# Which block of an attention group is summed by GpSimd and which goes to TensorE alone, and when the sum is closed

## The chip, the cores and the metric

The kernel runs on one core of one Trainium2 chip. The metric is device time in microseconds (us) of one launch. The core has five engines that run their own instruction streams in order and wait for each other by semaphores: TensorE (PE; its weight loads are listed apart as PEld), VectorE (DVE), ScalarE (ACT), GpSimd (POOL) and SyncE (SP). SyncE and GpSimd issue the data transfers (DMA) that matter here.

## The reference, cut to what matters

For each of 8 frames of 2048 rows and 256 channels: multi-head attention with 8 heads of 32 channels and a mask, then a feed-forward part, with three layer norms and residuals.

```
scores = einsum('fnhd,fmhd->fhnm', q, k) / sqrt(D)
scores = where(adj > 0, scores, -1e9)
attn   = softmax(scores, axis=-1)
t      = einsum('fhnm,fmhd->fnhd', attn, v)
x      = layernorm(x + t)
x      = layernorm(x + relu(x @ w1 + b1) @ w2 + b2)
out    = layernorm(x_in + x)
```

What the change touches is the softmax's denominator: for each query and head, the sum of the exponentials over all 2048 keys.

## The kernel before, in words

**Groups and blocks.** The 2048 queries of a frame are cut into 4 chunks of 512 (`qc`), the 8 heads into 2 halves of four (`g`), and the 2048 keys into 16 blocks of 128 (`mb`). A group is (`f`, `qc`, `g`); it has 16 blocks, and all groups together have 1024 blocks, the list `items`. The groups follow each other as qc 0 g 0, qc 0 g 1, qc 1 g 0, and so on.

**One block.** `scores` (L215, L218) makes the scores of 128 keys and 512 queries for four heads on TensorE, into two double banks of PSUM, and VectorE adds the mask while it moves them to a tile `p` of 128 x 2048 in SBUF. `exponentials` (L222) applies exp in place on ScalarE. `values` (L234) multiplies the tile by the values on TensorE and adds up over the 16 blocks in a bank. The main loop issues, at block t: `advance(t, 1)`, which runs pieces of side work; the exponentials of block t+1; the scores of block t+2; the values of block t; and `add_up` of block t. So a side piece stands ahead of the scores and the values of its block in TensorE's order. `advance` isn't called at block 0 of a group, and gives out one PSUM bank, so one TensorE piece, a block.

**The denominator.** The sum over the keys of a block is a product with a matrix of ones on TensorE. To save such products, the 16 tiles of a group are first added into a few. `add_up` does that with two means. The blocks in `POOLED` are added by GpSimd, one after the other, into the tile of block 0 (L256). The blocks in the two chains of `MOVED` are added by accumulating transfers that GpSimd issues (L253), each into the first tile of its chain; a later transfer of a chain adds into the same tile and waits until the earlier one has landed. One block, `ALONE`, is added to nothing. So four tiles, the terms, are left. `denominator` multiplies each with ones (L292, four matmuls a term, all accumulating in one bank), two terms in one piece of side work and two in the next; its result is turned (L299) and inverted. It begins `SUM` blocks after the last block of the group, that is in a block of the next group.

**What follows.** After g 1 of a chunk, `outcome` divides (L328, L329) and adds the input rows by an accumulating transfer (L317). `tail` follows: a norm, the feed-forward (L394, L397, L399, L405, L415, L417), a second norm with GpSimd's L339 and L341, the residual by an accumulating transfer (L343), and the third norm. Its GpSimd operations stand in the same queue as `add_up`'s. They start at blocks counted from `SUM`. Other side work prepares the next frame: rows are turned (L152), written to DRAM and loaded again (L182), and projected to queries, keys and values (L172, L197).

**Buffers.** The tiles `p` come from a pool of 11; a tile is reused when the values, the sum that takes it in, or the ones-product has read it. Side work is ordered by a list of start blocks and due times, and the whole order is fixed when the program is built.

In the last group of the program the blocks in `ENDED` aren't added by GpSimd but go to TensorE as terms of their own.

Of the kernel before, what the change touches and what calls it, by code (L numbers as in the profile page):

```python
# [55 lines left out]
def fast_path(ctx, tc, cst, x, adj, out, RS):  # L56
# [30 lines left out]
    def bank(dt=F32):  # L87
        shape = [P, CH] if dt == F32 else [P, 2, CH]
        if state["side"] is not None:
            i = 1 - state["side"]  # L90
            return ps_x[i].tile(shape, dt, name=f"x{i}")
        i = state["turn"]
        state["turn"] = (i + 1) % 5
        pool = ps_s[i] if i < 3 else ps_x[i - 3]
        return pool.tile(shape, dt, name=f"s{i}" if i < 3 else f"x{i - 3}")
# [109 lines left out]
    PT, O, OT, RC = {}, {}, {}, {}  # L205
# [33 lines left out]

    POOLED = (0, 3, 6, 8, 11, 13, 15)
    MOVED = ((1, 4, 7, 10), (2, 5, 9, 12))
    ALONE = 14

    ENDED = (13, 15)
    SUM = 4

    def add_up(item):
        f, qc, g, mb = item  # L250
        for chain in MOVED:
            if mb in chain[1:]:
                nc.gpsimd.dma_start(PT[f, qc, g, chain[0]], PT.pop(item), accum_op=ALU.add)  # L253
        if mb in POOLED[1:] and not ((f, qc, g) == items[-1][:3] and mb in ENDED):
            first = PT[f, qc, g, POOLED[0]]
            nc.gpsimd.tensor_tensor(first, first, PT.pop(item), ALU.add)  # L256
# [22 lines left out]

    def denominator(f, qc, g):  # L280
        grp = (f, qc, g)
        terms = [PT.pop((f, qc, g, ALONE))] + [PT.pop((f, qc, g, chain[0])) for chain in MOVED + (POOLED,)]
        if (f, qc, g) == items[-1][:3]:
            terms[3:3] = [PT.pop((f, qc, g, b)) for b in ENDED]
        yield BANK
        ps = bank()
        for n, term in enumerate(terms):
            if n == 2:
                yield BANK
            for h in range(4):  # L290
                r = D * h
                nc.tensor.matmul(ps[r:r + D, :], cst["ones"], term[:, h, :], start=(n == 0), stop=(n == len(terms) - 1))  # L292
        dT = op.tile([P, CH], F32, name="dT")
        nc.scalar.copy(dT, ps)  # L294
        yield 1
        yield BANK
        ps = bank()
        for j in range(TPC):
            nc.tensor.transpose(ps[:, j * P:(j + 1) * P], dT[:, j::TPC], ident)  # L299
        if g == 0:  # L300
            RC[f, qc] = op.tile([P, TPC, H], F32, name="rc")
        rc = RC[f, qc]
        den = ps.rearrange("p (j c) -> p j c", c=P)[:, :, ::D]
        nc.vector.reciprocal(rc[:, :, 4 * g:4 * g + 4], den)
        nc.vector.tensor_tensor(RS[:, 0], RS[:, 0], den, ALU.add)
        nc.vector.tensor_tensor(RS[:, 1], RS[:, 1], den, ALU.min)
        if g == 1:
            begin = items.index((f, qc, g, LAST)) + SUM + 2
            start(begin, outcome(f, qc) if (f, qc) != (F - 1, NCK - 1) else finish(f, qc), begin)

    def outcome(f, qc):
        yield ROOM
        state["tails"] += 1
        xin = x[f, qc * CH:(qc + 1) * CH, :].rearrange("(p j) c -> p j c", p=P)
        y = yp.tile([P, TPC, C], F32, name="y")
        yield from divide(f, qc, y)
        nc.gpsimd.dma_start(y, xin, accum_op=ALU.add)  # L317
        begin = items.index((f, qc, 1, LAST)) + SUM + 2
        start(begin + 10, tail(f, qc, y, xin), begin + 26)
# [13 lines left out]
    def tail(f, qc, y, xin):  # L333
        yield from norm(y)
        yield from feed_forward(y)
        yield 1
        z = y
        yield from norm(z)
        nc.gpsimd.tensor_tensor(z, z, rows(cst["g2r"]), ALU.mult)  # L339
        yield 1  # L340
        nc.gpsimd.tensor_tensor(z, z, rows(cst["be2r"]), ALU.add)  # L341
        yield 1
        nc.gpsimd.dma_start(z, xin, accum_op=ALU.add)  # L343
        yield 7
        yield from norm(z)
        nc.sync.dma_start(out[f, qc * CH:(qc + 1) * CH, :].rearrange("(p j) c -> p j c", p=P), z)
        state["tails"] -= 1
# [20 lines left out]
    def finish(f, qc):  # L368
        y = yp.tile([P, TPC, C], F32, name="y")
        xr, xb = state["rows"], take([P, TPC, C], F32)  # L370
        yield from divide(f, qc, y)
        nc.vector.tensor_tensor(y, y, xr, ALU.add)
        norm_halves(y)
        nc.vector.tensor_tensor(xb, xr, rows(cst["be2r"]), ALU.add)
        yield from feed_forward(y)
        z = y
        norm_halves(z)
        for h in range(0, TPC, 2):
            nc.vector.tensor_tensor(z[:, h:h + 2], z[:, h:h + 2], rows(cst["g2r"])[:, h:h + 2], ALU.mult)
            nc.vector.tensor_tensor(z[:, h:h + 2], z[:, h:h + 2], xb[:, h:h + 2], ALU.add)  # L380
        norm_halves(z)
        dst = out[f, qc * CH:(qc + 1) * CH, :].rearrange("(p j) c -> p j c", p=P)
        for h in range(0, TPC, 2):
            nc.sync.dma_start(dst[:, h:h + 2], z[:, h:h + 2])
# [37 lines left out]
    def start(t, gen, due):  # L422
        fill.append([t, gen, 1, due])
        fill.sort(key=lambda e: e[3])
# [88 lines left out]
    for t, (f, qc, g, mb) in enumerate(items):  # L513
        if mb == 0 and t:
            state["side"] = 1 - state["side"]
        if g == 1 and mb % 2 and (f + 1 < F or qc + 1 < NCK):
            load_mask(f + (qc + 1) // NCK, (qc + 1) % NCK, mb // 2)
        if f + 1 < F:
            for what, *which in NEXT.get((2 * qc + g, mb), []):
                due = t + MB // 2 if what is turn else items.index((f + 1, 0, which[1], which[0] * TPC)) - LEAD - 1  # L520
                start(t, what(f + 1, *which), due)
        if t == len(items) - MB // 2:
            state["rows"] = take([P, TPC, C], F32)
            nc.sync.dma_start(state["rows"], x[f, qc * CH:(qc + 1) * CH, :].rearrange("(p j) c -> p j c", p=P))
        if mb:
            advance(t, 1)

        if t + 1 < len(items):
            exponentials(items[t + 1])
        if t + LEAD < len(items):  # L530
            nf, _, ng, nmb = items[t + LEAD]
            t0 = t
            while (nf, nmb // TPC, ng) not in V:
                advance(t0, 1)
                t0 += 1
            scores(items[t + LEAD])
        values(items[t])
        add_up(items[t])
        if mb == LAST:
            start(t + SUM, denominator(f, qc, g), t)  # L540
    t = len(items)
# [129 lines left out]
def kernel(  # L671
# [56 lines left out]
    nc.gpsimd.memset(RS[:, 1], 1.0)  # L728

    fast_path(tc, cst, x, adj, out, RS)  # L730


# [49 lines left out]
```

## Time and profile before

| | |
|---|---|
| time | 3436.56 us, median of 3 runs (3432.72 to 3441.2) |
| span of the profiled run | 3439.1 us |
| mean granted TensorE clock | 0.990 |
| groups, blocks | 64, 1024 |
| accumulating transfers p<-p (L253) | 384 of 1024 KB, 10.1 us in the median from issue to landing |
| adds on GpSimd (L256) | 382, 4.9 us each |
| ones-products (L292) | 2064 matmul instructions, 244.9 us busy |

A row of the profile's groups reads: line, engine, operation, what it writes and reads, how often; then the busy time, the mean of one in ns, and after the bar the engine's idle time ahead of the group's instructions and what ended it. A row of the waits reads: engine, tile and line, then what it waited for, the sum in us, how often, and the longest. A row of a timeline reads: start and duration in us, engine, line, operation, what it writes and reads, how many were merged, and in brackets the idle time ahead of it. A transfer issued by GpSimd occupies it for the issue alone; the landing comes later.

### The profile page before, as it was taken

Reading aid. Unit: us, or ns where it says so; the run is one execution under the profiler, and the core shown is the slowest. Engines: PE = TensorE matmul, PEld = TensorE weight load, DVE = VectorE, ACT = ScalarE, POOL = GpSimd, SP = SyncE. Lnnn points to the kernel's source line nnn. Section 1 sums busy time; section 2 is a strip of 40 time slices with the busy share of each in tenths; the row PEclk is TensorE's granted clock in tenths of the full one; section 3 lists DMA queues with packets and bytes.
Section 4 is the critical chain, followed back from the end, with each engine's and each line's share of the span. In section 5 each row is a group of like instructions: output and inputs, shape, how many; then the busy total and the mean of one; then the engine's idle time right before and its main releaser. Section 6 shows DMA issues by size and latency. Waiting matters only on the chain. (4 is left out here: it accounts for less than half of the span.)

```text
span 3439.1 us, 54435 instructions
## 1 busy us (share of the span) xinstructions
PE 3179.1 (92%) x22036; PEld 1038.5 (30%) x22036; DVE 2731.0 (79%) x3203; ACT 2426.5 (71%) x1937; POOL 2586.7 (75%) x1357
## 2 busy tenths in 40 slices
PE   6989999999999999999999999999999999998995
PEld 5222332223322233222332323223332223322222
DVE  4788768887788877888788887888768887689885
ACT  3677767776677767777677776777767777677774
POOL 0577768887688776888678876787777877788885
PEclk8999999999999999999999999999999999999998
DMA  8678768778678777778777777687776787777774
GB/s 309 149 156 173 173 161 174 158 159 200 142 167 184 154 180 153 163 172 181 170 154 170 161 175 178 141 180 172 164 179 140 160 187 167 169 158 154 151 162 99
DMA packets 149298, 575.99 MB, mean 167 GB/s; under 512 B 14608, under 2 KB 67344, under 8 KB 99888
## 3 DMA queue, kind: packets, MB, share of 16 engines
q0 software_dynamic: 64560, 435.85, 63.2%
q1 hardware_dynamic: 83664, 135.30, 11.4%
q8 instruction: 174, 2.85, 0.3%
q10 hardware_dynamic: 816, 1.31, 0.1%
q14 instruction: 84, 0.69, 0.1%
HBM read 131.99 MB, written 37.75 MB: 49 GB/s over the span
## 5 line engine op out<-in xcount | busy, mean ns | idle before, releaser
L218 DVE TENSOR_TENSOR p<-s,mask 128x1024 f32<-128x1024 f32 x2048 | 2410.0, 1219 | 568.5 <-PE s L215 343.9
L222 ACT ACTIVATE p<-p 128x2048 f32<-128x2048 f32 x1024 | 1956.6, 1911 | 484.6 <-DVE p L218 371.2
L256 POOL TENSOR_TENSOR p<-p 128x2048 f32<-128x2048 f32 x382 | 1851.8, 4898 | 385.9 <-ACT p L222 383.4
L215 PE MATMUL s<-qT,kT 32*128 32x512 f32 x8192 | 1169.8, 641 | 184.9 <-DVE p L218 174.6
L234 PE MATMUL x<-p,v 128*32 128x512 f32 x8192 | 1091.8, 605 | 2.3 <-ACT p L222 2.3
L253 POOL DMA_DIRECT2D p<-p x384 | 385.6, 1024 | 376.0 <-DMA p<-p 188.4
L215 PEld LDWEIGHTS s<-qT,kT 32*128 32x128 f32 x8192 | 320.5, 183 | 822.3 <-DVE p L218 756.2
L234 PEld LDWEIGHTS x<-p,v 128*32 128x32 f32 x8192 | 161.1, 108 | 780.1 <-issue 211.5
L172 PE MATMUL x<-in,wqkv 128*128 128x512 f32 x472 | 235.2, 621 | 14.7 <-DMA in<-xd 14.1
L292 PE MATMUL x<-p,ones 128*32 128x512 f32 x2064 | 244.9, 592 | 1.9 <-DMA p<-p 1.9
L274 ACT ACTIVATE y<-y,nb,rs 128x256 f32<-128x256 f32 x372 | 219.0, 590 | 7.1 <-POOL nb L271 7.1
L263 DVE BATCH_NORM_STATS2 st<-y 128x6 f32<-128x256 f32 x372 | 155.4, 418 | 0.0
L172 PEld LDWEIGHTS x<-in,wqkv 128*128 128x128 f32 x472 | 80.2, 189 | 170.9 <-issue 112.7
L294 ACT COPY dT<-x 128x512 f32<-128x512 f32 x64 | 37.4, 585 | 126.3 <-PE x L292 126.3
L415 PE MATMUL x<-w2s,hT 128*128 128x256 f32 x504 | 125.5, 392 | 0.1
L405 PE MATMUL x<-turned,w1s 128*128 128x512 f32 x248 | 123.0, 618 | 0.0
L197 PEld LDWEIGHTS x<-wqkv,in 128*128 128x128 f32 x896 | 104.2, 191 | 47.0 <-issue 41.1
L197 PE MATMUL x<-wqkv,in 128*128 128x128 f32 x896 | 114.9, 281 | 0.0
L292 PEld LDWEIGHTS x<-p,ones 128*32 128x32 f32 x2064 | 66.8, 110 | 156.4 <-issue 151.0
L415 PEld LDWEIGHTS x<-w2s,hT 128*128 128x128 f32 x504 | 90.6, 189 | 62.0 <-issue 50.3
L268 POOL TENSOR_TENSOR rs<-rs,mhalf 128x4 f32<-128x4 f32 x93 | 96.2, 1035 | 7.8
L200 ACT COPY v<-x 128x512 f32<-128x512 f32 x58 | 33.9, 585 | 93.6 <-PE x L197 93.6
(114 smaller groups left out, 1467.6 us busy)
## 6 DMA issues: line engine op xcount, KB each, us to landing
p<-p POOLq DMA_DIRECT2D x384, 1024.0 KB, 10.1
mask<-md SPq DMA_DIRECT2D x248, 128.0 KB, 6.2
y<-in_x_dram POOLq DMA_DIRECT2D x62, 512.0 KB, 6.1
in<-xd SPq DMA_DIRECT2D x59, 512.0 KB, 10.9
p<-in_adj_dram SPq DMA_DIRECT2D x16, 1024.0 KB, 9.6
out_dram<-y SPq DMA_DIRECT2D x31, 512.0 KB, 6.4
in<-in_x_dram SPq DMA_DIRECT2D x29, 512.0 KB, 10.4
xd<-in SPq DMA_DIRECT2D x28, 512.0 KB, 9.2
```

What stands on the lines that cost most here:

```text
L172: nc.tensor.matmul(ps, wqkv[:, a, k0:k0 + P], xT[:, a, :], start=(a == 0), stop=(a == 1))
L197: nc.tensor.matmul(ps[:, j * P:(j + 1) * P], xT[:, a, j * P:(j + 1) * P], wqkv[:, a, 2 * C + g * P:2 * C + (g + 1) * P], start=(a == 0), s ...
L215: nc.tensor.matmul(ps2[half][:, j, :], KT[f, mb // TPC, g][r:r + D, (mb % TPC) * P:(mb % TPC + 1) * P], QT[f, qc, g][r:r + D, :], start=Tr ...
L218: nc.vector.tensor_tensor(pt[:, 2 * half:2 * half + 2, :], ps, MK[f, qc, mb // 2][:, mb % 2, None, :].to_broadcast([P, 2, CH]), ALU.add)
L222: nc.scalar.activation(PT[item], PT[item], AF.Exp, scale=1.0 / math.sqrt(D))
L234: nc.tensor.matmul(O[grp][r:r + D, :], V[f, mb // TPC, g][:, mb % TPC, r:r + D], PT[item][:, h, :], start=(mb == 0), stop=(mb == LAST))
L253: nc.gpsimd.dma_start(PT[f, qc, g, chain[0]], PT.pop(item), accum_op=ALU.add)
L256: nc.gpsimd.tensor_tensor(first, first, PT.pop(item), ALU.add)
L263: nc.vector.bn_stats(st, t[:, j, :])
L274: nc.scalar.activation(t[:, j, :], t[:, j, :], AF.Identity, bias=nb[:, j:j + 1], scale=rs[:, j:j + 1])
L292: nc.tensor.matmul(ps[r:r + D, :], cst["ones"], term[:, h, :], start=(n == 0), stop=(n == len(terms) - 1))
L415: nc.tensor.matmul(ps[:, (j - jj) * C:(j - jj + 1) * C], hT[:, d, j * P:(j + 1) * P], w2s[:, d, :], start=(d == 0), stop=(d == 1))
```

## The change

```diff
-    POOLED = (0, 3, 6, 8, 11, 13, 15)
-    MOVED = ((1, 4, 7, 10), (2, 5, 9, 12))
-    ALONE = 14
-
-    ENDED = (13, 15)
-    SUM = 4
+    POOLED = (0, 3, 5, 8, 10, 12, 14)
+    MOVED = ((1, 4, 7, 11), (2, 6, 9, 13))
+    ALONE = 15
+
+    ENDED = (12, 14)
+    SUM = 3
...
-        terms = [PT.pop((f, qc, g, ALONE))] + [PT.pop((f, qc, g, chain[0])) for chain in MOVED + (POOLED,)]
+        terms = [PT.pop((f, qc, g, ALONE))] + [PT.pop((f, qc, g, chain[0])) for chain in (MOVED[0], POOLED, MOVED[1])]
         if (f, qc, g) == items[-1][:3]:
-            terms[3:3] = [PT.pop((f, qc, g, b)) for b in ENDED]
+            terms[2:2] = [PT.pop((f, qc, g, b)) for b in ENDED]
```

The last block of a group, 15, now goes to TensorE alone, and GpSimd's last add is that of block 14. The chains of transfers are cut anew: one ends in block 11 instead of 10, the other in block 13 instead of 12. With `SUM` 3 the ones-products stand in blocks 2 and 3 of the next group instead of 3 and 4, and what is counted from `SUM` moves one block earlier with them. The order of the terms changes: before it was the lone block, first chain, second chain, GpSimd's sum; now it is the lone block, first chain, GpSimd's sum, second chain. The purpose is to close the sum of a group earlier, and so to hand back the tiles of its first blocks earlier. The number of adds, transfers and products stays the same.

## The prediction

> **What bounds the kernel now.** I read the page's busy shares first, then its costliest groups, then the waits, then the GpSimd and TensorE timelines of one group.
>
> ```profile
> PE 3179.1 (92%) x22036; PEld 1038.5 (30%) x22036; DVE 2731.0 (79%) x3203; ACT 2426.5 (71%) x1937; POOL 2586.7 (75%) x1357
> ...
> L218 DVE TENSOR_TENSOR p<-s,mask 128x1024 f32<-128x1024 f32 x2048 | 2410.0, 1219 | 568.5 <-PE s L215 343.9
> ...
> L256 POOL TENSOR_TENSOR p<-p 128x2048 f32<-128x2048 f32 x382 | 1851.8, 4898 | 385.9 <-ACT p L222 383.4
> ...
> p<-p POOLq DMA_DIRECT2D x384, 1024.0 KB, 10.1
> ```
>
> TensorE leads, but a block has two paces. A block without a side piece takes two VectorE adds, 2 x 1.22 = 2.44 us (2.5 in the trace); a block with a side piece (ones-products, projection, feed-forward) takes 3.8 to 4.0 us of TensorE: 1.14 scores + 1.07 values + 1.7 to 1.9 of the piece. The 53.7 us average of 64 groups is a sum of such blocks with little idle. So moving a piece gains or loses nothing of itself; only a wait in TensorE's or VectorE's order changes the time. GpSimd is next: does it deliver sums in time?
>
> ```profile
> POOL p L253 <- DMA p<-p: 188.4, 43, 6.2
> ...
> PE x L292 <- DMA p<-p: 1.9, 1, 1.9
> ```
>
> GpSimd waits 188 us for the accumulate transfers of its own chains, but the ones-products (L292) nearly never wait. To see how much slack hides this, GpSimd in frame 2, group (qc 1, g 0):
>
> ```profile
> 1029.33 4.58 POOL L256 TENSOR_TENSOR p<-p 128x2048 f32<-128x2048 f32 x1 [3.15 <-ACT p L222]
> ...
> 1044.34 0.90 POOL L317 DMA_DIRECT2D y<-in_x_dram  x1
> 1044.96 1.19 POOL L253 DMA_DIRECT2D p<-p  x1
> 1045.54 5.21 POOL L256 TENSOR_TENSOR p<-p 128x2048 f32<-128x2048 f32 x1
> 1050.05 1.52 POOL L253 DMA_DIRECT2D p<-p  x1
> 1055.38 0.85 POOL L253 DMA_DIRECT2D p<-p  x1 [3.81 <-DMA p<-p]
> 1055.96 4.86 POOL L256 TENSOR_TENSOR p<-p 128x2048 f32<-128x2048 f32 x1
> 1060.48 2.66 POOL L339 TENSOR_TENSOR y<-y,g2r 128x1024 f32<-128x1024 f32 x1
> 1062.79 1.19 POOL L253 DMA_DIRECT2D p<-p  x1
> 1063.40 2.98 POOL L341 TENSOR_TENSOR y<-y,be2r 128x1024 f32<-128x1024 f32 x1
> 1065.73 5.17 POOL L256 TENSOR_TENSOR p<-p 128x2048 f32<-128x2048 f32 x1
> 1070.23 1.52 POOL L343 DMA_DIRECT2D y<-in_x_dram  x1
> 1070.99 9.90 POOL L256 TENSOR_TENSOR p<-p 128x2048 f32<-128x2048 f32 x2
> ```
>
> and TensorE at the start of the next group:
>
> ```profile
> 1069.21 1.07 PE L234 MATMUL x<-p,v 128*32 128x512 f32 x8
> 1070.94 1.14 PE L215 MATMUL s<-qT,kT 32*128 32x512 f32 x8 [0.67 <-DVE p L218]
> 1072.02 1.07 PE L234 MATMUL x<-p,v 128*32 128x512 f32 x8
> 1072.90 1.90 PE L292 MATMUL x<-p,ones 128*32 128x512 f32 x16
> ...
> 1076.68 1.90 PE L292 MATMUL x<-p,ones 128*32 128x512 f32 x16
> ```
>
> The exponential of block 15 ended at 1063.37 (call it E15). The last transfer (block 12, issued 1062.79) landed at 1070.33, 7.0 after E15; its term, the third, starts at 13.3 after E15: 6 us of slack. The last add (block 15, 1070.99 to 1076.5) ends 13.1 after E15, for the fourth term at 14.3 (1.90/2 = 0.95 a term): 1 us of slack.
>
> **What the Trainium skill says.** *DMA: Bandwidth & Descriptors*, section "SWDGE vs HWDGE vs iDMA": an accumulate in a transfer goes through GpSimd's software path alone, and that has one queue. The trace agrees: two accumulates issued at 1083.13 and 1083.75 landed after 6.9 and 13.7 us, one behind the other. *TensorE: Matmul & The Clock Gate*, "The mechanism": matmuls start and end strictly in program order, so a late ones-product holds the scores behind it; no run here shows the hold at length (1.9 us once, above). *GPSIMD Engine Reference*, "Elementwise": a two-input add of 2048 fp32 columns takes 4497 ns; here 4534 at least, 4868 in the median, and I use the trace.
>
> **The change, part by part.** Same counts: 6 adds, 6 accumulate transfers and 4 terms of 4 matmuls a group. (a) Ones-products move from blocks 3 and 4 to 2 and 3, and all that is queued behind them one block earlier: cost 0 by the additive block times. (b) The buffer that comes free latest relative to its next use: the new order lets every block's buffer be reused 8 blocks on, where some had 6 and 7. No row of the waits shows VectorE held by it beyond about 20 us in all, so I give it 0 to 10 us. (c) Both chains now have gaps of 3 and 4 blocks instead of some 3 and 3. (d) The second chain ends in block 13, not 12, and its term is the fourth, in block 3.
>
> Part (d) decides. For a group like the one above I set E3 = 0. With the pieces a block earlier, E4, E5 ... are the old intervals from E4 on: 4.1, 7.2, 10.2, 13.1, 16.0, 18.4, 20.9, 23.6, 26.1, 28.6, 31.2, and E15 = 33.7 (1065.87 - 1032.14). GpSimd's new order is add 3, transfer 4, a normalisation's four small operations, add 5, L317, transfers 6 and 7, add 8, transfer 9, add 10, L339, transfer 11, L341, add 12, L343, transfer 13, add 14. Add 5 starts 0.6 after E5, as add 6 does now behind the same operations, and ends 12.3. L317 issues then and lands 5.6 later as now, 17.9. Transfer 6, queued behind it, takes the 4.9 us that a queued accumulate takes in this stage (median over 112): 22.8. Transfer 9 must wait for it (same chain): issued 23.3. From there the operations follow back to back as from 1055.38 to 1070.23 above, with the same members: add 10 at 23.9, L343 at 23.9 + (1070.23 - 1055.96) = 38.2, transfer 13 at 39.0, add 14 from 39.6 to 45.
>
> L343's half megabyte lies directly ahead of transfer 13 in the one queue: it lands about 5.9 after issue (6.3 median, 5.8 least), at 44.1. Transfer 13 lands 4.9 (this stage) to 6.0 (median of the queued ones in g 1 groups, where mask loads share the engines) later: 49.0 to 50.1, so 15.3 to 16.4 after E15. The terms now start one block (1072.02 - 1069.21 = 2.8) earlier: 6.7, 7.6, 10.5, 11.4 after E15. Term 2 needs transfer 11 (issued 30.7, landed 37.6, 3.9 after E15): no wait. Term 3 needs add 14 (11.3): 0.8. Term 4 needs transfer 13: in all 3.9 to 5.0, I take 4.6; from the outside, 0.8 if L343 costs the queue nothing (39.0 + 6.9 alone) and 6.4 if both run at the slowest of their kind. Queued behind term 4 are the scores of block 5, and VectorE, ScalarE and the values wait for those. VectorE has one block of work at most, which it would have had anyway; it already waits for TensorE in these blocks, so the wait is paid in full.
>
> How many groups: those with g 0 have this tail work on GpSimd and short blocks at the end. qc 0, 1, 2 of 8 frames, less the first (no tail yet), and qc 3 of the last frame: 24. In the 8 with qc 2 a projection lengthens a late block, and their last add lags 6.7 instead of 7.8 now, so 3.5 each. 16 x 4.6 + 8 x 3.5 = 102 us. In g 0, qc 3 the last blocks take 4 us, so GpSimd catches up (transfer 13 about 7 after E15, term 4 at 14.7). In g 1 groups blocks are long too: transfer 13 about 5 to 11 after E15 for a term at 13 or later.
>
> Gains: VectorE's L417 waits 22.3 us in all for GpSimd's L399; in the new g 1 groups L399 ends some 4 us ahead of need. Under half of those waits is on the path (VectorE has 0.9 us to spare in such blocks): 9 us. The end of the program: term 6 waits for the last transfer both before and after; 0. Sum: 3436.6 + 102 - 9 = 3530.
>
> **The rivals.** (1) A small stall: transfer 13 overtakes or shares with L343, 0.8 to 1 us x 24 = 22, less 9: 3450. For it: the page states no order of completion across engines; against: queued transfers landed one by one. Chance 0.14. (2) Faster: GpSimd is far enough ahead after the rearranged chains (188 us of its waits go) that no term waits, and the waits of (b), L417 and part of the reload stalls go: 3436 - 22 = 3415. For it: those waits are there; against: GpSimd's idle time isn't the path's, and L343 stays ahead of transfer 13. Chance 0.10. (3) Larger: 24 x 6.4 = 154, without gains: 3590. For it: some queued transfers in g 1 groups took 9.4; chance 0.10. My forecast: 0.66.
>
> **How the numbers follow.** The time is the forecast's, 3530. Range: 3455 (nearly rival 1) to 3580 (nearly rival 3) leaves out about 0.2. Faster than 0.3%: 0.10 (rival 2). Slower: forecast, rival 3 and most of rival 1: 0.86. Same: 0.04.
>
> **What would show it.** In the changed profile: the weight load or matmul of L292 waiting for DMA p<-p, some 24 times 3 to 6 us, about 100 us in all; it appears at block 3 of g 1 groups, after L343 and transfer 13 issued back to back; L417's waits for L399 shrink; GpSimd's waits for its own transfers fall below 188; plain blocks stay at 2.5. I am wrong if transfer 13 lands within 11.4 us of E15, or if L292's waits show and the group's length doesn't grow by them.

## The result and the profile after

The changed kernel takes 3565.95 us (median of 4 runs, 3560.19 to 3569.85) against 3435.72 of the kernel before on the same chip (4 runs, 3432.72 to 3441.2): ratio 1.0376, 95% interval 1.0354 to 1.0398, so some 130 us slower. The forecast was 3530, in a range of 3455 to 3580: direction and cause as forecast, the loss 37 us larger than the 93 forecast.

The page of the changed kernel, the lines that answer to those of before:

```profile
PE 3232.3 (91%) x22036; PEld 1040.8 (29%) x22036; DVE 2731.4 (77%) x3203; ACT 2426.6 (68%) x1937; POOL 2583.0 (73%) x1357
...
L256 POOL TENSOR_TENSOR p<-p 128x2048 f32<-128x2048 f32 x382 | 1834.9, 4803 | 595.2 <-ACT p L222 510.7
...
L292 PE MATMUL x<-p,ones 128*32 128x512 f32 x2064 | 262.3, 619 | 80.7 <-DMA p<-p 70.5
...
p<-p POOLq DMA_DIRECT2D x384, 1024.0 KB, 9.5
```

Counts are those of before, and VectorE, ScalarE and GpSimd are as busy in us as before. Two rows moved. The ones-products L292 now stand idle for `DMA p<-p`. And TensorE is busy 53 us longer (3232.3 against 3179.1) with the same 22036 matmuls, so some of them run slower. The mean granted TensorE clock is 0.975 (0.990 before).

The waits of the changed kernel (what waited and for what, sum in us, times, longest):

```profile
PEld x L292 <- DMA p<-p: 93.0, 25, 5.0
...
PE x L292 <- DMA p<-p: 70.5, 23, 4.1
...
POOL p L253 <- DMA p<-p: 54.0, 26, 4.3
```

The first two rows are one wait seen twice: the weight load of a term waits for its tile, and the matmul behind it waits along. They aren't to be added. The first begins while the matmuls of term 3 still run, the second, 70.5 us in 23 waits, is TensorE's idle time alone. GpSimd's waits for its own chains fell from 188.4 to 54.0 us, and the kernel is slower all the same.

GpSimd in the group that the prediction showed (frame 2, qc 1, g 0); block 15's exponential ends at 1088.47, which is E15:

```profile
1082.83 2.69 POOL L339 TENSOR_TENSOR y<-y,g2r 128x1024 f32<-128x1024 f32 x1
1085.14 1.20 POOL L253 DMA_DIRECT2D p<-p  x1
1085.77 2.98 POOL L341 TENSOR_TENSOR y<-y,be2r 128x1024 f32<-128x1024 f32 x1
1088.10 5.16 POOL L256 TENSOR_TENSOR p<-p 128x2048 f32<-128x2048 f32 x1
1092.60 1.51 POOL L343 DMA_DIRECT2D y<-in_x_dram  x1
1093.16 1.84 POOL L253 DMA_DIRECT2D p<-p  x1
1093.74 5.88 POOL L256 TENSOR_TENSOR p<-p 128x2048 f32<-128x2048 f32 x1
```

The chain of work that ended last, in the same stretch (start, us, what):

```profile
1092.60 0.56 POOL y L343
1093.16 11.31 DMA p<-p
1104.48 0.04 issue
1104.52 1.93 PE x L292 x8
```

L343's residual is issued just ahead of transfer 13. The transfer takes 11.3 us and lands at 1104.48, 16.0 after E15, while GpSimd's last add has been done since 1099.6. TensorE at that time:

```profile
1099.67 1.06 PE L292 MATMUL x<-p,ones 128*32 128x512 f32 x8 [0.25 <-POOL p L256]
1104.52 1.93 PE L292 MATMUL x<-p,ones 128*32 128x512 f32 x8 [3.78 <-DMA p<-p]
1106.38 2.09 PE L215 MATMUL s<-qT,kT 32*128 32x512 f32 x8
1108.40 1.94 PE L234 MATMUL x<-p,v 128*32 128x512 f32 x8
```

Term 3 takes 1.06 us. Term 4, after the idle time, takes 1.93 for the same eight instructions, and the scores and values behind it also take nearly double. The windows say why (us, busy time of PE, PEld, DVE, ACT, POOL, granted clock, DMA share, GB/s):

```profile
1100.80:1104.50 3.70, 0.00 (x0) 0.00 (x0) 0.12 (x1) 0.00 (x0) 3.53 (x4) 0.91 0.64 146
1104.50:1108.00 3.50, 3.48 (x16) 0.72 (x16) 0.00 (x0) 1.48 (x2) 1.54 (x1) 0.50 0.00 0
...
1112.00:1116.00 4.00, 4.00 (x34) 1.27 (x31) 3.63 (x5) 3.13 (x4) 2.90 (x1) 1.00 0.95 184
```

In 3.7 us of nothing the granted clock falls to 0.50 (0.91 is the mean of the first window: the fall came 0.7 us before the wait ended), and it is back at 1.00 in the last window: the wait has a second part, paid after it ends.

### The profile page after: what moved, and what is told of

Read it like the earlier page. It is cut to its first block, busy times and chain, and to the rows that moved or that the text cites. A ratio compares the mean times of both kernels' runs of the same rounds, so it can differ in the third digit from the quotient of the medians.

```text
span 3560.5 us, 54566 instructions
## 1 busy us (share of the span) xinstructions
PE 3232.3 (91%) x22036; PEld 1040.8 (29%) x22036; DVE 2731.4 (77%) x3203; ACT 2426.6 (68%) x1937; POOL 2583.0 (73%) x1357
## 4 chain that ended last, share of the span: by engine, by line
PE 54%; DMA 17%; POOL 11%; DVE 10%; issue 5%; ACT 1%; DVEq 0%; POOLq 0%; ACTq 0%; SPq 0%
PE s L215 19%; PE x L234 13%; DMA p<-p 13%; DVE p L218 9%; PE x L172 6%; PE x L292 5%; POOL p L256 5%; PE x L415 3%; PE x L405 3%; PE x L197 2%; DMA xd<-in 2%; POOL y L341 2%; POOL y L339 2%; DMA in<-xd 1%; PE x L394 1%
## 5 line engine op out<-in xcount | busy, mean ns | idle before, releaser
L215 PE MATMUL s<-qT,kT 32*128 32x512 f32 x8192 | 1189.3, 651 | 175.0 <-DVE p L218 167.6
L234 PE MATMUL x<-p,v 128*32 128x512 f32 x8192 | 1102.9, 611 | 0.0
L253 POOL DMA_DIRECT2D p<-p x384 | 402.3, 1093 | 200.3 <-ACT p L222 118.4
L292 PE MATMUL x<-p,ones 128*32 128x512 f32 x2064 | 262.3, 619 | 80.7 <-DMA p<-p 70.5
L274 ACT ACTIVATE y<-y,nb,rs 128x256 f32<-128x256 f32 x372 | 219.0, 590 | 3.0 <-POOL nb L271 3.0
L292 PEld LDWEIGHTS x<-p,ones 128*32 128x32 f32 x2064 | 63.3, 111 | 248.0 <-issue 126.9
L415 PE MATMUL x<-w2s,hT 128*128 128x256 f32 x496 | 123.6, 392 | 0.0
L267 POOL TENSOR_SCALAR rs<-mv 128x4 f32<-128x4 f32 x93 | 17.9, 193 | 123.3 <-DVE mv L264 121.0
L415 PEld LDWEIGHTS x<-w2s,hT 128*128 128x128 f32 x496 | 89.1, 189 | 61.6 <-issue 50.3
```

Of the source, the lines that this page charges most:

```text
L215: nc.tensor.matmul(ps2[half][:, j, :], KT[f, mb // TPC, g][r:r + D, (mb % TPC) * P:(mb % TPC + 1) * P], QT[f, qc, g][r:r + D, :], start=Tr ...
L234: nc.tensor.matmul(O[grp][r:r + D, :], V[f, mb // TPC, g][:, mb % TPC, r:r + D], PT[item][:, h, :], start=(mb == 0), stop=(mb == LAST))
L274: nc.scalar.activation(t[:, j, :], t[:, j, :], AF.Identity, bias=nb[:, j:j + 1], scale=rs[:, j:j + 1])
L415: nc.tensor.matmul(ps[:, (j - jj) * C:(j - jj + 1) * C], hT[:, d, j * P:(j + 1) * P], w2s[:, d, :], start=(d == 0), stop=(d == 1))
```

## The experiments

Ratios are to the kernel before, timed on the same chip (its median there 3441 to 3448). "Terms" are the four ones-products, counted from 1. "The waiting groups" are the 23 groups of g 0 in which the changed kernel waits for transfer 13; times after E15 are medians over them, where nothing else is said. A block's length is taken from the start of its values to the start of the next block's. In the changed kernel transfer 13 is issued at 4.6 after E15 and lands at 15.4 (16.0 in the group above).

**1. L343 behind transfer 13.** The changed kernel with L343 issued one block later:

```diff
-        yield 1
+        yield 2
         nc.gpsimd.dma_start(z, xin, accum_op=ALU.add)
-        yield 7
+        yield 6
```

> The changed kernel with one edit: the residual transfer L343 is issued a block later, behind transfer 13 instead of ahead of it. Theory (transfer 13 is late because L343 lies ahead of it in the one queue): it lands some 5 us earlier after the end of block 15's exponential, about 10 to 11 instead of 15.9; L292's waits for DMA p<-p fall from 163 us to under 20, the wait of about 1 us for the sum of GpSimd stays; 3430 to 3455 us. Rival (GpSimd issues transfer 13 too late in any case, as its adds lag by two to three blocks): the landing moves by the 0.6 us of the issue alone, and the time stays above 3540.

Measured: 3482.62, ratio 1.0097 (1.008 to 1.0113), between the theory and the rival. Transfer 13 now lands 13.0 after E15 instead of 15.4, and term 4 waits less (`PEld x L292 <- DMA p<-p`, the row that is 93.0 above, is 35.7 us in 25, 2.6 at most; the 163 of the expectation adds up the two rows of one wait). TensorE in the group with the longest of these waits:

```profile
1085.95 1.07 PE L292 MATMUL x<-p,ones 128*32 128x512 f32 x8 [0.32 <-POOL p L256]
1088.73 1.06 PE L292 MATMUL x<-p,ones 128*32 128x512 f32 x8 [1.72 <-DMA p<-p]
```

What follows: 2.8% of the 3.8% go with the half megabyte ahead of transfer 13. But the landing didn't move to where no term waits. The transfer is still issued 4.2 after E15, since L339, L341 and add 12 stand ahead of it, and takes 8.6 with L343 right behind it. After a wait of 1.7 the term runs at full pace (1.06).

**2. Transfer 13 left out.** Block 13's exponentials are missing from the denominator of every group here, so the second chain ends in block 9:

```diff
-            if mb in chain[1:]:
+            if mb == 13 and mb in chain:
+                PT.pop(item)
+            elif mb in chain[1:]:
```

> The changed kernel without transfer 13: the exponentials of block 13 are left out of the denominator, all else is the same. Theory (the whole loss hangs on that one transfer's landing): the fourth term doesn't wait, the granted clock is back to 0.99, and the time is 3425 to 3445 us. Rival (ones-products a block earlier, or the other end of the side work's shift, cost something of their own): 3460 us or more.

Measured: 3447.63, ratio 0.9998 (0.9989 to 1.0006). The ones-products' waits for transfers are gone (0.3 us), and TensorE's own for the add come to 1.5 us; the first six blocks of the next group take 18.5 us again (18.5 before, 24.6 in the changed kernel; medians for qc 0). What follows: nearly all of the loss hangs on this one transfer. All else that the change moved sums to about nothing, gains and losses together.

**3. A busy TensorE during the wait.** In the waiting groups 16 matmuls with a matrix of zeros (a tile filled once at the start) stand ahead of term 4, adding zeros into the same bank:

```diff
+            if n == len(terms) - 1 and g == 0 and (qc < 3 and 4 * f + qc > 1 or f == F - 1):
+                for h in 4 * [0, 1, 2, 3]:
+                    r = D * h
+                    nc.tensor.matmul(ps[r:r + D, :], zeros, terms[n - 1][:, h, :], start=False, stop=False)
```

> The changed kernel, with 16 matmuls by a matrix of zeros ahead of the fourth term in the 23 groups that wait there: about 3.8 us of TensorE work that fits into the wait and adds zero to the sum. Theory (beside the wait itself, the clock that TensorE is granted after standing idle costs 1.5 us a stall): transfer 13 lands as before, the fourth term and the scores behind it run at 592 ns a matmul instead of 1060, clock 0.985 or more, and the time falls by 25 to 40 us to about 3530. Rival (the excess over the wait is VectorE and ScalarE starting anew from empty): no change, or slower by what the zero products stick out, 3565 to 3600 us.

Measured: 3544.59, ratio 1.0273 (1.0256 to 1.029). TensorE in this kernel, where L296 are the products with zeros and L299 the terms (two instructions a matmul):

```profile
1106.55 3.62 PE L296 MATMUL x<-p,zeros 128*32 128x512 f32 x32
1110.06 1.07 PE L299 MATMUL x<-p,ones 128*32 128x512 f32 x8
```

The term comes no earlier than in the changed kernel (16.3 after E15 against 15.5) but takes 1.07, and the clock of the window 1104 to 1112 is 1.00. In none of the 23 groups does the clock fall at term 4. What follows: (1.0376 - 1.0273) x 3441 = 35 us of the loss, give or take 10 (both ratios' intervals combined), go with the clock after the waits.

**4. The new sets, summed one block later:** `SUM = 4` in the changed kernel.

> The changed kernel with SUM 4 again: the new sets of blocks and order of terms stay, the ones-products and the side work counted from SUM stand one block later. L343 then comes behind transfer 13. Theory (a landing against a block): transfer 13 lands about 13 us after block 15's exponential, the fourth term starts at 14.3, so no wait; 3420 to 3440 us. Rival (a last transfer in block 13 is too late for either place): some 2 us in each of 23 groups, 3480 us or more.

Measured: 3464.5, ratio 1.0042 (1.0028 to 1.0056), short of the 3420 to 3440 expected. Term 4, now due at about 14.2, hardly waits (the weight loads of L292 for transfers 12.9 us in all). Instead there is a wait that is larger than in any other run here (24.1 us in experiment 6, 3.0 in the kernel before):

```profile
DVE p L218 <- DMA p<-p: 50.8, 35, 4.1
```

What follows: VectorE needs tiles again by then that transfers of the chains still read. With these sets the sum can't simply go back to its later place. How much of the 0.4% this wait makes was not measured apart.

**5. The earlier sum alone:** `SUM = 3` in the kernel before, its sets unchanged.

> The kernel before with SUM 3 alone: old sets of blocks (last transfer in block 12, last add that of block 15), ones-products and side work one block earlier. Theory (each term's landing against its block): transfer 12 lands about 7 us after block 15's exponential, in time; the last add ends about 13, and the fourth term, now at 11.4, waits for it about 1.7 us in some 23 groups, too short for the clock to fall: 35 to 45 us slower than the kernel before. Rival (the move of the ones-products is the harm, whatever the last transfer): over 100 us slower, as in the changed kernel.

Measured: 3460.22, ratio 1.0031 (1.0018 to 1.0043), some 11 us where 35 to 45 were expected.

```profile
PEld x L292 <- POOL p L256: 44.7, 23, 2.7
```

Here the old last add, block 15's, ends 13.0 after E15 for a term due at 11.6: term 4 starts 0.3 to 2.0 late in 23 groups, 29 us in all. It was partly paid back: the blocks of g 0, qc 3 that wait for reloaded rows, 15 us too long in all before, are all 4.0 us here (see experiments 10 and 11). What follows: the new sets were made for a real need. Without them the earlier sum waits for GpSimd's add; with them it waits longer, for a transfer.

**6. Block 12 in the chain, 13 on GpSimd.** The changed kernel with the last transfer one block earlier:

```diff
-    POOLED = (0, 3, 5, 8, 10, 12, 14)
-    MOVED = ((1, 4, 7, 11), (2, 6, 9, 13))
+    POOLED = (0, 3, 5, 8, 10, 13, 14)
+    MOVED = ((1, 4, 7, 11), (2, 6, 9, 12))
...
-    ENDED = (12, 14)
+    ENDED = (13, 14)
```

with the terms in the order lone block, first chain, second chain, GpSimd's sum. 

> The changed kernel with the second chain ending in block 12 again: adds of blocks 3, 5, 8, 10, 13, 14, transfers 4, 7, 11 and 6, 9, 12, block 15 alone, SUM 3, GpSimd's sum as the last term. Theory: transfer 12 issues ahead of L343 and lands about 9 to 10 us after block 15's exponential, before its term at 10.5; the last add ends at 11.6 to 14 for a term at 11.4: waits of 0.2 to 2 us a group; from no change to 40 us slower than the kernel before, so at least 80 us faster than the changed kernel. Rival (GpSimd's tail operations make any last block late): within 40 us of the changed kernel.

Measured: 3456.86, ratio 1.0025 (1.0015 to 1.0035). The last transfer, issued just before E15, lands 10.3 after it, the last add ends at 11.4, and terms 3 and 4 start at 10.8 and 11.6: the wait is nearly gone (weight loads for transfers 20.8 us in all, up to 4.3). The longest block of g 0, qc 3 is still 6.3 to 8.4 us where the others are 4.0. What follows: where the last transfer stands, not the number of transfers, makes the large wait; something else keeps the sum from gaining.

**7. The tail's GpSimd work later:** `yield 3` put ahead of L339 in the changed kernel, so that L339, L341 and L343 all come three blocks later and transfer 13 stands ahead of them.

> The changed kernel with the tail's two GpSimd operations L339 and L341, and L343 behind them, three blocks later, so behind transfer 13. Theory (two halves: L343 ahead in the queue, and GpSimd's 5.6 us of tail work ahead of transfer 13's issue): transfer 13 issues 5 to 6 us earlier and lands 7 to 9 us after block 15's exponential, the last add ends about 8 us after it; no term waits, L292's waits for DMA p<-p are below 15 us in all; within 15 us of the kernel before. Rival (the service of the queue at the group's start is what is slow): the landing stays over 11.4, and 20 us or more remain.

Measured: 3455.58, ratio 1.0022 (1.0009 to 1.0035). Transfer 13 is issued 0.3 before E15 and lands at 9.3; the terms start at 7.0, 7.8, 10.8, 11.6 and none waits. What follows: with experiment 1, the way from 15.4 to 9.3 splits into L343 ahead (2.4 us) and GpSimd's late issue behind its tail work (3.7). Still no gain: g 0, qc 3 keeps a block of 7.7 to 11.6 us in each of the seven frames that prepare a next one.

**8. The same delay on the old sets:** the kernel before, `SUM = 3`, `yield 5` ahead of L339.

> The kernel before with SUM 3 (old sets) and the tail's L339, L341 and L343 behind the group's last add. Theory: with 5.6 us of tail work gone from ahead of it, the last add ends 7 to 8 us after block 15's exponential and no term waits; the reload of turned rows in the fourth g 0 group doesn't wait either, as with the old sets and SUM 3 alone, which is worth 10 to 15 us; 10 to 25 us faster than the kernel before. Rival (the delayed third norm collides with the feed-forward's pieces on ScalarE and GpSimd in the g 1 groups): no faster than the kernel before.

Measured: 3525.86, ratio 1.024 (1.0226 to 1.0254). No ones-product waits, and the time is 2.1% longer than in experiment 5 all the same:

```profile
DVE y L418 <- POOL y L400: 99.6, 23, 6.0
PEld x L416 <- DVE y L418: 81.1, 22, 5.1
```

(These are L417, L399 and L415 of the kernel before, one line on.) The rival came true. What follows: the work put off belongs to the end of one chunk's tail, and L399 to the feed-forward of the next chunk's tail, later in the same queue. With the delay L399 comes too late, and block 14 of the g 1 groups of qc 0 to 2 takes 5.0 to 11.0 us from frame 1 on, instead of 4.0. A wait taken off one deadline came back on another, larger. Which of GpSimd's pieces in between hands the delay on wasn't traced.

**9. Only L341 and L343 later:** the kernel before, `SUM = 3`, and `yield 6` for `yield 1` between L339 and L341.

> The same, with L341 and L343 alone behind the last add and L339 where it was. Theory: the last add ends 9 to 10 us after block 15's exponential, in time for a term at 11.6, so the same gain, 10 to 25 us faster than the kernel before. Rival: as above, no faster.

Measured: 3486.6, ratio 1.0121 (1.0106 to 1.0137). Again no ones-product waits; L417 waits 54.6 us for L399, and ScalarE's norm (L274) 77.5 for GpSimd's L271. What follows: the same as from 8. At these two delays the old sets leave no place for this work; the new ones do at theirs (experiment 7).

**10 and 11. Blocks 5 and 6 exchanged.** Both have the changed kernel's sets but for these two blocks. 10 also has the `yield 3` of experiment 7; 11 has the exchange alone.

```diff
-    POOLED = (0, 3, 5, 8, 10, 12, 14)
-    MOVED = ((1, 4, 7, 11), (2, 6, 9, 13))
+    POOLED = (0, 3, 6, 8, 10, 12, 14)
+    MOVED = ((1, 4, 7, 11), (2, 5, 9, 13))
```

> The changed kernel with the tail's L339, L341 and L343 three blocks later, as in the run with the late tail, and with blocks 5 and 6 exchanged between the second chain and GpSimd's adds: transfers 4, 7, 11 and 5, 9, 13, adds 3, 6, 8, 10, 12, 14. Theory: transfer 13 still lands 8 to 10 us after block 15's exponential, so no term waits; and as transfers 6 and 7 no longer issue back to back where the turned rows are written to DRAM, that write lands in about 4 instead of 11 us and the projection that waited 4 us a frame for the reload doesn't wait: 15 to 30 us faster than the kernel before. Rival (the reload's wait has another cause, or comes back elsewhere): as the run with the late tail, 0 to 12 us slower than the kernel before.

> The changed kernel with blocks 5 and 6 exchanged alone, the tail where the change has it. Theory: the reload's wait goes (some 25 us less), the wait for transfer 13 behind L343 stays: 2.5 to 3.3 per cent slower than the kernel before, and L292's waits for DMA p<-p stay over 100 us. Rival (the exchange also mends transfer 13's lateness): under 1 per cent slower.

Measured: 10 takes 3421.95 against 3441.11, ratio 0.9942 (0.9928 to 0.9955), faster than both kernels. 11 takes 3517.31, ratio 1.0227 (1.0211 to 1.0243). The ones-products of 10, from the view of their line (idle time ahead of them, by what ended it; L342 and L418 are L341 and L417, one line on):

```profile
  issue: 147.2, 492
  POOL y L342: 4.8, 16
  POOL rs L267: 1.8, 6
  DVE y L418: 0.8, 1
```

No transfer is in the list. Of 11, the waits:

```profile
PEld x L292 <- DMA p<-p: 88.6, 25, 4.8
```

What follows: the exchange leaves the wait for transfer 13 nearly as it was (88.6 against 93.0), yet saves 1.5%, a little more than expected. About half of that, 25 of 46 us, is saved elsewhere (for the rest see what stays open, below): in g 0, qc 3 the write of turned rows `xd<-in` (L164), which the reload and the next frame's projections wait for, took 11.0 to 12.2 us in the changed kernel (7 frames), 7.9 to 9.6 before, and 4.0 to 6.2 in 10 and 11 (3.5 to 6.0 in 5). In the changed kernel transfers 6 and 7 are issued 0.6 apart, some 4 us ahead of the write, and are both in flight beside it; in 11 transfer 5 lands within 0.3 us of the write's issue, and 7 is issued just behind it (frame 2). The blocks that waited are 4.0 us again. This fits *DMA: Bandwidth & Descriptors* of the Trainium skill, section "Queues, rings and completion order": each transfer engine takes turns between the queues that have work for it, so a transfer of another queue shares, it doesn't pass. A trial with the two transfers spread but the rest untouched is just what 11 is; that the engines' turns are the mechanism was not measured apart.

## Why the prediction was right, and where its size was off

1. *Transfer 13 behind L343.* Right, in order and in number: forecast to land 15.3 to 16.4 after E15; medians over the frames 15.9, 15.4 and 14.5 for qc 0, 1 and 2 (for qc 2 the prediction took some 1.1 less). Experiments 1 and 7 show the cause, and that it has two parts: the residual ahead and the late issue.
2. *The terms.* Forecast 6.7, 7.6, 10.5 and, unstalled, 11.4; measured 7.0, 7.8, then 11.1 (add 14 ends at 11.1; forecast 11.3). Term 2 doesn't wait, term 3 waits little, term 4 waits for the transfer. Right.
3. *The size of the wait.* 16 x 4.6 + 8 x 3.5 = 102 was forecast. Against the kernel of experiment 7, where no term waits, term 4 starts 3.5 to 4.8 late in qc 0, 3.6 to 4.4 in qc 1, 2.2 to 4.4 in qc 2 (median 2.9; 6.1 in the last frame) and 4.7 in the last group of that kind: 89 us in all. That is the 70.5 of the waits' row and 18.5 more, most of it because term 3 is itself late, by 0.6 in the mean (0.8 was forecast). The groups are 23, not 24: in frame 0 the tail work comes only in qc 2, so two groups are free of it where the prediction left out one. g 1 groups and the other g 0, qc 3 are free of it, as said.
4. *"The wait is paid in full".* This step failed in size: it is paid with more. The first six blocks of the next group are 134.5 us longer in those 23 groups than in experiment 7, 45 more than the 89. Where the clock doesn't drop, the same excess is 9: 42 for 33 us of lateness in experiment 1, and 109 for 100 in experiment 3. So some 36 are the clock; experiment 3's time gives 35 by another way. The prediction read the clock nowhere. *TensorE: Matmul & The Clock Gate* of the Trainium skill, section "HAM oscillation — how this bites in real kernels", puts the limit of an idle gap at about 3.4 us. This case doesn't show such a limit for the gap itself. In the changed kernel waits of 2.38 to 4.08 us were followed by a drop in 20 of the 23 groups, waits of 2.03, 2.23 and 3.00 by none; in experiment 11 a wait of 1.79 was followed by one, waits of 3.10 and 3.40 by none. Two waits of the changed kernel, in frames 0 and 5:

```profile
345.61 1.50 PE L292 MATMUL x<-p,ones 128*32 128x512 f32 x8 [2.38 <-DMA p<-p]
347.04 2.09 PE L215 MATMUL s<-qT,kT 32*128 32x512 f32 x8
...
2508.33 1.06 PE L292 MATMUL x<-p,ones 128*32 128x512 f32 x8 [3.00 <-DMA p<-p]
2509.33 1.14 PE L215 MATMUL s<-qT,kT 32*128 32x512 f32 x8
```

   What tells the cases apart is where the wait falls. In every trace the drops begin on one grid of 3.413 us, to 0.01 us. The wait of 3.00 lies across a line of that grid, at 2506.74, and so takes less than half of each of two windows; the wait of 2.38 takes most of one. Over all 13 traces (without the first 150 and the last 40 us) 106 windows at full clock were followed by a drop at their end: TensorE was idle for 58% or more of 105 of them, and for 52% of the one with the wait of 1.79. In the other 12276 windows it was idle for 58% at most. So some 2 us of idle time within one window went with a drop here, and not the length of the wait.
5. *"Both chains now have gaps of 3 and 4 blocks", and "moving a piece gains or loses nothing of itself".* The new gaps were given no cost, and that was wrong. The blocks of g 0, qc 3 from the sixth on are 25 us longer than in experiment 10 over seven frames; the same stall, taken as what the longest block has above 4.0, cost 15 before. That is 10 more, for the slower write beside transfers 6 and 7.
6. *The gains.* L417's waits for L399 went from 22.3 us to none in the list. The start and the end of the program are 5 us shorter, where nothing was forecast. All that neither 4 nor 5 counts in the blocks between is 18 us shorter than before, where 9 was forecast; this is what is left of the difference of the two spans, not a measurement of its own. What of it belongs to L417 was not measured apart.
7. *The sum.* The spans of the profiled runs differ by 3560.5 - 3439.1 = 121.4, which is 134.5 + 10 - 18 - 5; the medians of the timed runs differ by 130. Against the forecast of 102 - 9: 13 less for the waits, 45 more for what follows them, 10 more for the write, 14 more in gains.

The rivals: nothing came of the first (a small stall, 3450), since all 454 transfers of GpSimd's queue whose landing the trace tells landed in the order of issue, nor of the second (no wait, 3415), since GpSimd's add and transfer came as late as forecast. The third (3590) came nearer in size than the forecast, by luck: the waits weren't longer, they cost more each.

What stays open: experiment 11 saves more than the stall it removes. Of the 46 us between its profiled run and the changed kernel's, 25 are that stall; the 23 groups lose 107 instead of 134.5, since term 4 is 75 late instead of 89 and the clock drops in 14 of them instead of 20 (58 us at half clock instead of 99). By the windows of point 4 waits of nearly the same length can differ so by where they fall; whether the exchange moves them on the grid or chance does wasn't tried. Nor was it shown why the write slows beside transfers 6 and 7.

## What to carry to other kernels

When the order of a single in-order queue is rearranged, find what stands directly ahead of the transfer with the nearest deadline, however small, and when its engine gets to issue it; putting the obstacle off helps only if no later deadline inherits it (experiments 8 and 9). A TensorE wait of 2 to 4 us can cost more than itself: here 36 us for the clock over 23 waits, or some 1.6 each, though 3 of them saw no drop. Ask how much of one window of 3.4 us the idle time can fill, not only how long it lasts. Regrouped transfers also load the engines that other queues use, so look at who else has a transfer in flight when two of them become neighbours.

## What the runs showed of the hardware that was not expected

- Idle TensorE of 3.8 us: the next eight ones-products took 1.93 us instead of 1.06, at a granted clock of 0.50, for 3.4 or 6.8 us. Products with zeros in the gap kept it at 1.00.
- The drops begin on a grid of 3.413 us. Over 13 traces they followed windows of it in which TensorE was idle for 58% or more (once 52%), and none with less than 52%; a wait of 1.79 us was followed by a drop and one of 3.40 was not.
- Being first in the one queue of accumulating transfers doesn't give a transfer its time alone: with L343 right behind it, transfer 13 took 8.6 us, where the first of the two accumulates that the prediction looked at took 6.9. With L343 ahead it took 10.6 (11.3 in the group shown).
- In g 0, qc 3 a plain write of 512 KB from SyncE's queue took 4.0 to 6.2 us or 11.0 to 12.2, by what accumulating transfers were in flight.
